# The scan of a state-space layer inside a fused Perceiver kernel: the skip term as a diagonal matrix product, and an output projection in plain float32

## The chip, the cores and the metric

The kernel runs on one core of one Trainium2 chip. The metric is the device time of one execution in microseconds (us). The core has a matrix engine (TensorE, PE in the profile; its weight loads are a row of their own, PEld), a vector engine (VectorE, DVE), a scalar engine (ScalarE, ACT), GpSimd (POOL), and a queue, SyncE (SP), from which this kernel issues all its transfers. Each engine executes its own list of instructions strictly in order and waits on semaphores that the other engines raise. On-chip memory is SBUF; TensorE writes into PSUM.

## The reference, cut to what matters

The input x has 8 sequences of 64 rows of 512 numbers. Six residual blocks follow one another: cross attention over a context of 1601 rows with projections, a mamba block, a ternary linear layer, a second cross attention without weights, a causal self attention, and a gated ternary feed-forward layer. The change touches the mamba block alone:

```
proj = h @ W_in.T ;  x, gate = proj[..., :1024], proj[..., 1024:]
x    = silu(conv4(x))                      # "u" in the kernel
ts, Bm, Cm = rms of the parts of x @ W_x.T
dt   = softplus(ts @ W_dt.T + b_dt) ;  A = -exp(A_log)
for t:  state = state * exp(dt_t * A) + (dt_t * x_t) * B_t ;  y_t = sum_n state * C_t
y    = y + x * D
y    = y * silu(gate)
out  = y @ W_out.T                          # 1024 -> 512
```

The state has 16 components for each of 1024 channels. D is one number for each channel.

## The kernel before, in words

The first cross attention (lines 256 to 604) is by far the largest part and fills the first 2350 us or so. Two sequences make a pair, 128 rows. When a pair has its first cross attention, `chain` (line 782) does the other five blocks for it, as a generator. `run` (line 1312) spreads the chains of the first three pairs over the time of the first cross attention. The chain of the last pair (the "tail", `tail=True`) starts when no cross attention is left, and runs beside what is left of the third pair's chain. So from about 2367 us on there are two chains, that of the third pair and that of the last pair, and the order of their instructions on each engine is set by the framework's list scheduler when the program is built, not by hand.

In the tail all tiles lie in one pool, by tags with a fixed number of buffers: `s4` has 11 (tiles of 4 KB for each partition), `w2` has 12 (2 KB), `w2_r`, which the third pair uses, 8. A tile takes a free buffer of its tag when it is created and gives it back after its last use; a transfer into a tile therefore waits on SP for whoever used the buffer before. Everything behind it on SP waits too.

Mamba in the tail (`mamba`, line 810): channels lie on partitions, in eight chunks c of 128. A chunk's `u[:, c]` is 128 x 128 (channel x 2 sequences of 64 steps). `u` and `dt` and the gate `z` (all chunks of silu(gate), lines 862 to 866) are tiles of tag `s4`, held until the end of the block. Then for each chunk and each group of four state components (`CS = 4`, line 944 to 967):

- ACT makes four exponentials into one of two PSUM buffers `da` (L950),
- POOL (DVE in the first chunk) makes dt * u * B for four components at once, 128 x 512 (L956), into half of a tile `h8` of tag `s4`,
- DVE runs the recurrence (L959), and DVE, or POOL in the second group, multiplies with C (L960),
- PE adds the four components into the PSUM tile `yp[c % 2]` by products with the identity matrix (L962).

`finish(c)` (line 937) then closes a chunk: DVE makes u * D + y (L940), POOL multiplies with the gate (L941), and `mamba_out` (line 989) multiplies with W_out. That product is done in "halves": a float32 number is split into a rounded part and a remainder, both of type fp32r. ACT rounds (L105), DVE subtracts (L106), and `mm3` (line 763) loads the 512-KB pair of halves of W_out from a scratch array `d_wout` into an `s4` tile (L771) and makes three products, high x high (L777), low x high (L778), high x low (L780). They accumulate over the chunks in `wps`. At the end DVE adds the residual (L987).

`mm32` (line 757) is the other way of multiplying that the tail has: it loads a plain float32 matrix into a `w2` tile (L760) and makes one float32 product (L761). The tail's self attention uses it. The names in the profile leave out buffer numbers, so tag `s4` is `s`, the tag `a2` is `a`, and all PSUM tiles of this pool are `acc`.

The third pair's second cross attention runs beside the scan. Its last step, `values` (lines 1077 to 1120), multiplies the weights with the 1601 rows of the context, in 13 tiles; tiles come by six transfers of two (L1099) and a last one of 65 rows (L1101), and the products are L1104. ACT and DVE then close it (L1112, L1113, L1118, L1119). The last pair's second cross attention loads its context tiles into `s4` buffers (L1044).

Of the kernel before, what the change touches and what calls it, by code (L numbers as in the profile page):

```python
# [10 lines left out]
AF = mybir.ActivationFunctionType  # L11
ALU = mybir.AluOpType
# [4 lines left out]
P = 128  # L17
# [12 lines left out]
NCH = 8  # L30
NST = 16
# [47 lines left out]
class Kernel:  # L79
# [730 lines left out]
    def mamba(self, gi, x, xo):  # L810
        nc, i = self.nc, self.i
        tail = self.tail
        lt = self.lnT(x, P, hl=False, tg="a2")
        u = self.sb(self.tv if tail else "lu", [P, NCH, 2, T])
        gs = 2 if tail else 4

        def proj(m):
            w = self.sb(self.tw, [P, NC, P])
            nc.sync.dma_start(out=w, in_=i["W_inT"][m])
            ps = self.acc()  # L820
            for k in range(NC):
                nc.tensor.matmul(ps[:, :P], lhsT=w[:, k, :], rhs=lt(k, 0), start=k == 0, stop=k == NC - 1)  # L822
            return ps[:, :P].rearrange("p (b t) -> p b t", t=T)

        def gate(c, z):
            nc.scalar.copy(z[:, c % 4], proj(NCH + c))
            if c % gs == gs - 1:
                self.silu(z[:, c % 4 - gs + 1 : c % 4 + 1], self.sb("a2", [P, gs, 2, T]), self.sb("a2", [P, gs, 2, T]))

        for c in range(NCH):  # L830
# [4 lines left out]
            uc = u[:, c]  # L835
# [26 lines left out]
        if tail:  # L862
            z = self.sb(self.tv, [P, NCH, 2, T])
# [24 lines left out]
        def bcast(sh):  # L888
            bc = self.sb("bc", [P, 2, HS, 2, T])
            for a in range(2):  # L890
                r = a * NST + sh * HS
                nc.sync.dma_start(
                    out=bc[:, a].rearrange("p s b t -> p (s b t)"),
                    in_=self.bc_s[gi][r : r + HS].rearrange("r t -> (r t)")[None, :].to_broadcast([P, HS * P]),
                )
            return bc

        def scan(c, sh, bc):
            da = self.sb(self.td, [P, HS, 2, T])
            for s in range(HS):  # L900
                k = sh * HS + s
                nc.scalar.activation(da[:, s], dt[:, c], AF.Exp, scale=self.A[:, c, k : k + 1])
            nc.gpsimd.memset(da[:, :, :, 0:1], 0.0)
            du = dus[:, c]
            if sh == 0:
                nc.gpsimd.tensor_tensor(du, dt[:, c], u[:, c], ALU.mult)
            h = self.sb(self.ts, [P, HS, 2, T])
            nc.gpsimd.tensor_tensor(h, bc[:, 0], du[:, None].to_broadcast([P, HS, 2, T]), ALU.mult)

            yield SCAN_COST  # L910
            hf, df = h.rearrange("p s b t -> p (s b t)"), da.rearrange("p s b t -> p (s b t)")
            nc.vector.tensor_tensor_scan(hf, df, hf, 0.0, ALU.mult, ALU.add)
            yield SCAN_COST
            nc.gpsimd.tensor_tensor(h, h, bc[:, 1], ALU.mult)
            yield SCAN_COST
            y = da[:, 0]
            nc.vector.tensor_reduce(y.rearrange("p b t -> p (b t)"), h.rearrange("p s b t -> p (b t) s"), AX.X, ALU.add)
            if sh == 0:
                nc.vector.scalar_tensor_tensor(u[:, c], u[:, c], self.Dp[:, c : c + 1], y, ALU.mult, ALU.add)
            else:  # L920
                nc.gpsimd.tensor_tensor(u[:, c], u[:, c], y, ALU.add)
            yield SCAN_COST

        wps = None
        if tail:


            CS = 4
            bcs = [bcast(sh) for sh in range(nh)]
            das = [self.acc().rearrange("p (s b t) -> p s b t", s=CS, b=2) for _ in range(2)]  # L930
            for da in das:
                nc.scalar.activation(da[:, :, :, 0:1], self.ident[:, : 2 * CS].rearrange("p (s b o) -> p s b o", s=CS, o=1), AF.Copy, scale=0.0)
            hp = self.acc()
            yp = [self.acc() for _ in range(2)]
            wps = self.acc()

            def finish(c):
                uc = u[:, c]
                y = yp[c % 2][:, :P].rearrange("p (b t) -> p b t", t=T)
                nc.vector.scalar_tensor_tensor(uc, uc, self.Dp[:, c : c + 1], y, ALU.mult, ALU.add)  # L940
                nc.gpsimd.tensor_tensor(uc, uc, z[:, c], ALU.mult)  # L941
                self.mamba_out(c, uc, wps)

            for c in range(NCH):
                du = self.sb("du", [P, 2, T])
                nc.gpsimd.tensor_tensor(du, dt[:, c], u[:, c], ALU.mult)
                for k0 in range(0, NST, CS):
                    da = das[k0 // CS % 2]
                    for s in range(CS):
                        nc.scalar.activation(da[:, s, :, 1:], dt[:, c, :, 1:], AF.Exp, scale=self.A[:, c, k0 + s : k0 + s + 1])  # L950
                    bc, o = bcs[k0 // HS], k0 % HS
                    if o == 0:
                        h8 = self.sb(self.ts, [P, HS, 2, T])
                    h = h8[:, o : o + CS]
                    hf = h.rearrange("p s b t -> p (s b t)")
                    (nc.vector if c < HV else nc.gpsimd).tensor_tensor(h, bc[:, 0, o : o + CS], du[:, None].to_broadcast([P, CS, 2, T]), ALU.mult)  # L956

                    eng, hs = (nc.gpsimd, hf) if k0 == CS else (nc.vector, hp)
                    nc.vector.tensor_tensor_scan(hs, da.rearrange("p s b t -> p (s b t)"), hf, 0.0, ALU.mult, ALU.add)  # L959
                    eng.tensor_tensor(hf, hs, bc[:, 1, o : o + CS].rearrange("p s b t -> p (s b t)"), ALU.mult)  # L960
                    for s in range(CS):
                        nc.tensor.matmul(  # L962
                            yp[c % 2][:, :P], lhsT=self.ident, rhs=h[:, s].rearrange("p b t -> p (b t)"), start=k0 + s == 0, stop=k0 + s == NST - 1
                        )
                    if c and k0 == CS:
                        finish(c - 1)
                    yield 15 / 4
            finish(NCH - 1)
        else:
            for sh in range(nh):  # L970
                bc = bcast(sh)
                for c in range(NCH):
                    yield from scan(c, sh, bc)

            wps = self.acc()
            for c in range(NCH):
                if c % 4 == 0:
                    z = self.sb("a2", [P, 4, 2, T])
                gate(c, z)
                yield 0.8  # L980
                if c % 4 == 3:
                    uc = u[:, c - 3 : c + 1]
                    nc.vector.tensor_tensor(uc, uc, z, ALU.mult)
                    for k in range(c - 3, c + 1):
                        self.mamba_out(k, u[:, k], wps)
                        yield 1
# [531 lines left out]
```

## Time and profile before

| what | value |
|---|---|
| runs | 2663.71, 2667.18 (median), 2670.01 us |
| profiled execution | 2656.56 us, of which the span from first to last instruction is 2654.8 us |
| mean granted TensorE clock | 0.984 of full speed |
| busy over the span: PE, DVE, ACT, POOL | 95%, 63%, 51%, 49% |
| the chains' stretch with no first cross attention | 2367 us to the end |
| the last pair's scan | 2419 to 2502 us |
| last pair's L987 (mamba's end) | 2507.33 us |
| last instructions | L1306 of the third pair, after 2651.03 us |

Each row of a view gives a line of the kernel, the engine and the operation. In a timeline the first two numbers are the start in microseconds and the duration of the group; "x8" is the number of instructions in the group, and in brackets stands how long the engine was idle before and who ended that. A float32 product is two records of PE. The view by source line gives, after the count, the shortest, median and longest duration in nanoseconds, then the first and last start in microseconds. The stretch view gives busy microseconds for each engine, the granted clock, the share in which the 16 DMA engines were busy, and GB/s.

### The profile page before, as it was taken

To read this page: it belongs to the slowest core of one execution; us is meant where nothing else is said; L and a number is where in the kernel's file an instruction comes from. 1 tells how busy PE (TensorE), PEld (TensorE's weight loads), DVE (VectorE), ACT (ScalarE), POOL (GpSimd) and SP (SyncE) were. 2 spreads that over 40 slices of the span, in tenths; PEclk is the share of its full clock that TensorE was granted. 3 is DMA by queue.
4 is the path that set the end of the run, shared out by engine and by line. 5 is a ranking of instruction groups with operands and counts; after the bars stand their busy time and mean duration, and the time that the engine had idled before them with its cause. 6 is when DMAs were issued, how large, how long until landed. Compare 5 with 4: busy or idle time off the path is not lost. (4 is left out here: it accounts for less than half of the span.)

```text
span 2654.8 us, 43902 instructions
## 1 busy us (share of the span) xinstructions
PE 2513.8 (95%) x16192; PEld 2241.6 (84%) x16192; DVE 1671.4 (63%) x2747; ACT 1366.8 (51%) x3205; POOL 1291.8 (49%) x1305
## 2 busy tenths in 40 slices
PE   7999999999999999999999989999999999876888
PEld 6999899989989999987989888997898988864545
DVE  4545457665687766544567777554557687668755
ACT  4555554444556555544455555544456555445534
POOL 2445563463378655421356667632138467605420
PEclk9999999999999999999999999999999999987899
DMA  9799776675213244765425533654533543367676
GB/s 300 231 311 301 249 262 202 209 240 168 78 50 108 83 130 138 221 196 152 151 61 163 172 114 97 235 166 146 166 121 107 159 152 122 122 216 240 201 253 227
DMA packets 307672, 466.08 MB, mean 176 GB/s; under 512 B 91129, under 2 KB 187385, under 8 KB 302977
## 3 DMA queue, kind: packets, MB, share of 16 engines
q1 hardware_dynamic: 307456, 463.28, 54.2%
q8 instruction: 127, 2.08, 0.3%
q14 instruction: 89, 0.72, 0.1%
HBM read 389.66 MB, written 73.53 MB: 174 GB/s over the span
## 5 line engine op out<-in xcount | busy, mean ns | idle before, releaser
L367 PE MATMUL k_ps<-cxb,wk 128*128 128x384 f32 x2304 | 463.2, 343 | 28.3 <-ACT cxb L105 10.3
L338 PE MATMUL v_ps<-wv,cxb 128*128 128x256 f32 x3456 | 463.9, 282 | 1.3 <-DVE kt L109 1.2
L338 PEld LDWEIGHTS v_ps<-wv,cxb 128*128 128x128 f32 x3456 | 436.6, 189 | 16.7 <-issue 9.1
L367 PEld LDWEIGHTS k_ps<-cxb,wk 128*128 128x128 f32 x2304 | 399.2, 190 | 48.1 <-ACT cxb L105 10.7
L389 PE MATMUL s_ps<-q,kt 128*128 128x256 f32 (+1 forms) x2496 | 410.9, 298 | 9.6 <-DVE mx L396 4.2
L472 PE MATMUL o_ps<-S,v 128*128 128x256 f32 (+1 forms) x1664 | 409.9, 379 | 0.7 <-ACT v L341 0.4
L389 PEld LDWEIGHTS s_ps<-q,kt 128*128 128x128 f32 (+1 forms) x2496 | 338.9, 185 | 31.2 <-DVE mx L396 5.2
L460 POOL TENSOR_TENSOR ss<-ss,S 128x512 f32<-128x512 f32 x254 | 351.4, 1383 | 13.9 <-ACT S L431 0.9
L392 ACT COPY S<-s_ps 128x512 f32<-128x512 f32 (+1 forms) x448 | 241.8, 553 | 219.7 <-PE s_ps L389 216.2
L396 DVE TENSOR_TENSOR mx<-s_ps,mx 128x512 f32<-128x512 f32 x256 | 175.1, 684 | 285.0 <-ACT S L392 284.3
L472 PEld LDWEIGHTS o_ps<-S,v 128*128 128x128 f32 (+1 forms) x1664 | 298.7, 189 | 34.1 <-issue 1.4
L433 POOL TENSOR_TENSOR ss<-S,S 128x512 f32<-128x512 f32 x64 | 83.7, 1308 | 424.7 <-ACT S L431 377.0
L430 DVE TENSOR_TENSOR S<-S,m_ps 128x512 f32<-128x512 f32 (+1 forms) x448 | 257.8, 640 | 19.6 <-PE m_ps L416 19.4
L431 ACT ACTIVATE S<-S 128x512 f32<-128x512 f32 (+1 forms) x448 | 247.0, 600 | 44.3 <-DVE S L430 44.1
L108 ACT ACTIVATE kt<-k_ps,c_bk 128x384 fp32r<-128x384 f32 (+1 forms) x256 | 151.8, 593 | 211.9 <-PE k_ps L367 211.3
L109 DVE SCALAR_TENSOR_TENSOR kt<-k_ps,c_bk,kt 128x384 fp32r<-128x384 f32 (+1 forms) x256 | 160.7, 628 | 132.3 <-ACT kt L108 131.7
L341 ACT COPY v<-v_ps 128x256 f32<-128x256 f32 (+1 forms) x416 | 151.7, 368 | 162.2 <-PE v_ps L338 157.9
L338 PE MATMUL v_ps<-wv,cxt 128*128 128x256 f32 (+1 forms) x1536 | 208.6, 285 | 3.4 <-DVE kt L109 2.5
L338 PEld LDWEIGHTS v_ps<-wv,cxt 128*128 128x128 f32 (+1 forms) x1536 | 194.2, 177 | 12.9 <-DVE kt L109 3.8
L65 DVE TENSOR_TENSOR_SCAN a<-a,a 128x512 f32<-128x512 f32 x96 | 153.8, 1603 | 66.2 <-POOL a L65 66.0
L367 PE MATMUL k_ps<-cxt,wk 128*128 128x450 f32 x768 | 177.6, 374 | 0.3 <-ACT v L341 0.3
L65 ACT ACTIVATE a<-lv,c_A_log 128x128 f32<-128x128 f32 x384 | 123.2, 393 | 101.6 <-DVE a L65 100.8
(382 smaller groups left out, 3969.9 us busy)
## 6 DMA issues: line engine op xcount, KB each, us to landing
wo<-d_wo SPq DMA_DIRECT2D x127, 512.0 KB, 5.5
wk<-d_wk SPq DMA_DIRECT2D x63, 512.0 KB, 3.8
wv<-d_wv SPq DMA_DIRECT2D x31, 1024.0 KB, 5.8
cst<-in_ctxT_dram SPq DMA_DIRECT2D x96, 192.0 KB, 2.9
d_q<-q_t SPq DMA_DIRECT2D x32, 512.0 KB, 5.1
q<-d_q SPq DMA_DIRECT2D x64, 256.0 KB, 2.8
d_wo<-wo SPq DMA_DIRECT2D x32, 512.0 KB, 5.0
w<-d_wat SPq DMA_DIRECT2D x64, 256.0 KB, 3.3
```

Of the source, the lines that this page charges most:

```text
L65: return lambda *a, **k: self.tc.keep_in_program_order(f(*a, **k))
L108: nc.scalar.activation(hi, src, AF.Identity, bias=bias)
L109: eng.scalar_tensor_tensor(lo, src, bias, hi.bitcast(FP), ALU.add, ALU.subtract)
L338: nc.tensor.matmul(ps[:r], lhsT=cx[:, a, c, o : o + r], rhs=w[:, m, c, :], start=k == 0, stop=k == 11)
L367: nc.tensor.matmul(ps[:, :wd], lhsT=w[:, a, c, :], rhs=cx[:, m, c, :], start=k == 0, stop=k == 11)
L389: nc.tensor.matmul(sp[:r, gi, :], lhsT=kt[:, a, o : o + r], rhs=q[:, m, :], start=k == 0, stop=k == 2)
L392: nc.scalar.copy(s[:r, :n], sp[:r, :n])
L396: nc.vector.tensor_tensor(mx, sp, S[0] if len(S) == 1 else mx, ALU.max)
L430: nc.vector.tensor_tensor(sv, sv, ps[:r, 1:2].to_broadcast([r, w, 256]), ALU.add)
L431: nc.scalar.activation(sv, sv, AF.Exp, scale=ISC)
L460: nc.gpsimd.tensor_tensor(ss, ss, S[n], ALU.add)
L472: nc.tensor.matmul(ps[:, 0], lhsT=self.v[(b, j, t)][:r, hc : hc + P], rhs=S[t // 2][:r, t % 2], start=t == 0, stop=t == NT - 1)
```

## The change

Three things change, all in the last pair's mamba alone. First, eight diagonal matrices are made at the start of the block, chunk by chunk, by ACT from the identity and D, in a tile `dg` of tag `s4` (eight instructions of 128 x 128). Second, D u is added by PE: before a chunk's first group of states, a float32 product of the diagonal matrix with `u[:, c]` opens the sum in `yp`, and the sixteen products with the identity follow. `finish` no longer adds u * D on DVE and no longer multiplies on POOL; one DVE instruction multiplies y, read from PSUM, with the gate. Third, W_out is multiplied by `mm32`: no rounding on ACT, no subtraction on DVE, one float32 product in place of three fp32r products, and a 256-KB transfer into a `w2` tile in place of 512 KB into an `s4` tile. The first three pairs are computed as before.

```diff
@@ mamba
         gs = 2 if tail else 4
+        if tail:
+            dg = self.sb(self.tv, [P, NCH, P])
+            for c in range(NCH):
+                nc.scalar.activation(dg[:, c], self.ident, AF.Copy, scale=self.Dp[:, c : c + 1])
@@ finish
                 y = yp[c % 2][:, :P].rearrange("p (b t) -> p b t", t=T)
-                nc.vector.scalar_tensor_tensor(uc, uc, self.Dp[:, c : c + 1], y, ALU.mult, ALU.add)
-                nc.gpsimd.tensor_tensor(uc, uc, z[:, c], ALU.mult)
-                self.mamba_out(c, uc, wps)
+                nc.vector.tensor_tensor(uc, y, z[:, c], ALU.mult)
+                self.mm32(wps, uc.rearrange("p b t -> p (b t)"), i["W_outT"][c], c == 0, c == NCH - 1)
@@ the loop over groups of states
                     bc, o = bcs[k0 // HS], k0 % HS
+                    if k0 == 0:
+                        nc.tensor.matmul(yp[c % 2][:, :P], lhsT=dg[:, c], rhs=u[:, c].rearrange("p b t -> p (b t)"), start=True, stop=False)
@@
-                            yp[c % 2][:, :P], lhsT=self.ident, rhs=h[:, s].rearrange("p b t -> p (b t)"), start=k0 + s == 0, stop=k0 + s == NST - 1
+                            yp[c % 2][:, :P], lhsT=self.ident, rhs=h[:, s].rearrange("p b t -> p (b t)"), start=False, stop=k0 + s == NST - 1
```

## The prediction, made before the changed kernel ran

> **What bounds the kernel now.** I read the stretches first, to see which engine is full where the change acts.
>
> ```profile
> core 0: us, PE busy (x) PEld busy (x) DVE busy (x) ACT busy (x) POOL busy (x), PEclk, DMA share, GB/s
> 2425.00:2497.00 72.00, 60.73 (x375) 42.56 (x376) 68.37 (x100) 51.02 (x155) 51.83 (x53) 0.90 0.48 155
> 2497.00:2510.00 13.00, 8.21 (x41) 4.85 (x40) 7.32 (x15) 3.20 (x10) 3.33 (x5) 0.81 1.09 326
> ```
>
> In the scan DVE is busy 68.4 of 72 us (95%), PE 84%, ACT 71%, POOL 72%, the DMA engines 48%. In its last 13 us no engine is full, and the DMA engines are. So the scan is paced by DVE, and its end by something else. What that is, the chain of waits from 2485 to 2526 us says (start, length, what):
>
> ```profile
> 2494.58 1.03 PE acc L1104 x4
> 2495.61 0.02 issue
> 2495.63 7.73 DMA b_r<-in_ctxN_dram
> 2503.36 0.04 issue
> 2503.41 1.09 PE acc L1104 x2
> 2504.49 0.02 issue
> 2504.52 0.58 ACT b L1112
> 2505.10 0.21 ACT a L105
> 2505.31 0.04 issue
> 2505.35 0.80 PE acc L777
> ...
> 2506.87 0.44 PE acc L780
> 2507.31 0.02 issue
> 2507.33 0.69 DVE xr L987
> ...
> 2515.80 4.12 DMA w_r<-d_wat
> 2519.92 0.02 issue
> 2519.94 5.80 DMA w_r<-d_wat
> ```
>
> The third pair's last context tile (L1101) lands at 2503.36, one us after the last state sum (L962) ended at 2502.29. PE takes L1104 before the last W_out products, and ACT takes L1112 before the last rounding L105, so both chains wait for that tile. Later two loads of d_wat hold PE before the last pair's second cross attention, whose L1047 starts at 2526.93. Rows for the prices, from the views by source line:
>
> ```profile
> L106 DVE TENSOR_TENSOR a<-s,a x8: 273/292/1179, 2445.8 to 2505.7; 128x128 fp32r<-128x128 f32 x8
> L940 DVE SCALAR_TENSOR_TENSOR s<-s,c_Dp,acc x8: 314/322/349, 2438.7 to 2502.3; 128x128 f32<-128x128 f32 x8
> L836 ACT ACTIVATE s<-xpad,c_conv_b,c_conv_w x8: 481/494/495, 2375.7 to 2384.1; 128x128 f32<-128x128 f32 x8
> ```
>
> **The change part by part**, with the order that the two programs' instructions have on each engine.
>
> *Diagonal matrices.* Eight ACT instructions, 128 x 128, SBUF to SBUF with a scale per partition. No such row exists. Below: four casts of the same size take 0.90 us together (L65, 2359.13), so 8 x 0.225 = 1.8 us. Above: L836, with scale and bias, is 0.49 alone, 3.9 us. Four exponentials of 126 columns with a scale per partition (L950) take 1.57 us in a row, 0.39 each: I take 3.1 us. They stand on ACT ahead of the block's first L118, and wait for the third pair's last W_out product, since the pool's memory is free only then; SP's first weight load waits for the same and starts at 2367.42. So they end at 2369.2, 2370.5 or 2371.3, and L118 (2369.51) comes 0, 1.0 or 1.8 us later; behind it wait the layer norm, its transposes and all projections. What hides that: u is complete at 2391.12 (L748), but its last product L850 stands on PE behind L1047, which waits for a context tile until 2391.24 and ends at 2392.3. So up to 1.1 us costs nothing. On SP one 256-KB load of d_wat now stands before that tile's transfer (issued 2385.29, 5.91 us to landing, DMA share 1.06): 0.25 MB at 375 GB/s is 0.7 us. These overlap; I take **+0.7** (0 to +1.8).
>
> *The scan.* DVE loses eight L106; six lie before the last exponentials (2497.8): 0.28 + 1.18 + 0.87 + 0.42 + 0.29 + 0.29 = 3.3 us. The new product reads PSUM and SBUF as L960 does, 0.69 us for 512 columns; L940 of the same 128 columns is 0.32, and I leave the product there. A gain of 0.2 more from one operand fewer is possible. Bounds: 6 x 0.28 = 1.7 us if the long ones were long only because POOL was in the way and the next instruction inherits that, 3.9 us with all eight. I take **-3.4**.
>
> The Trainium skill's page "SBUF — State Buffer", section "Who interferes with whom", says that a DVE instruction with two SBUF inputs and a GpSimd one that reads SBUF exclude each other, and one with a PSUM input does not. L106 (two SBUF inputs: 273 to 1179 ns) against L940 (one in PSUM: 314 to 349 ns) agrees. By the rule the whole 3.3 goes; by the short row alone it would be 1.7.
>
> ACT loses 8 x 0.28, POOL 8 x 0.45 us; neither paces. PE changes three fp32r products of 512 columns (0.23 apart: 2.1) for one float32 product: eight records of L761 take 3.44 us, two make a product, 0.86. The diagonal is a 128-column float32 product, 0.23 (L822: eight records, four products, in 0.98). Per chunk 0.86 + 0.23 - 0.69 = +0.4, in all +3.2 us, hidden by PE's 72.0 - 60.7 = 11.3 us of idle time; without that cover +3.2. W_out's 2 MB instead of 4 come early, in `w2` buffers, so `h8` has seven buffers to itself where it shared eight with W_out; POOL's wait of 3.7 us for L780 (L956, 2447.43) goes. SP's attnT loads (eight) and d_ffn (four), which came before 2412, move behind W_out's, into the scan and its end.
>
> *The end of the scan.* Let E be the end of the last exponentials, 2497.76 before. L1101 now stands on SP behind a load that takes `dt`'s buffer and so waits for E, then an attnT and one more load: issue at about E + 1.1, where it was E - 2.1. Context loads from 2478 to 2508 land after 3.6 us in the median case, this one took 7.73: E + 4.7 to E + 8.8, before E + 5.6. The other b_r loads have 4.9: I take E + 6.0, **+0.4** (-0.9 to +3.2). From its landing to L987 it was 3.97 us. Now L1104 1.09, then the last W_out product, which has its operands: 0.86 at full clock, 1.72 at half, and some 0.15 until DVE starts: 2.1 to 3.0. PE was at half clock there (L777, L778 of 0.80, 0.72 against 0.40). I take **-1.1** (-1.9 to -1.0).
>
> *Behind it.* The last pair's ffn products (eight) now stand before the third pair's d_wat products, and of those only the 12 with loads made early and two groups more (four loads) stand before L1047, where seven loads had to land. Four loads' landing is at 2519.9 in the chain, the seventh 2525.7. But the d_wat loads are issued about 2 us later (behind ffn and four attnT loads), and ffn's result must go through another layer norm (L794 at 2519.33 to L736 at 2523.56 before). So L1047 comes 0 to 3.6 us earlier beyond what it inherits; I take **-2.0**. The end comes after a stretch bound by PE and loads; I let the sum through.
>
> Sum: 0.7 - 3.4 + 0.4 - 1.1 - 2.0 = **-5.4 us** against the profiled execution, 2656.56 to 2651.2. The median of the runs lies 10.6 us above that execution; the same step gives 2667.18 - 5.4 = **2661.8 us**. Within 0.2% (5.3 us) a measurement of this kernel can hardly tell a change from none, its three runs being 6.3 us apart.
>
> **Rivals.**
>
> A, the forecast: most terms come out. Its own range, with the ends of the terms that go together, is -10 (0 - 3.9 - 1.9 - 0.9 - 3.6) to -3, 2657 to 2664.
>
> B, the context tile holds the end and nothing is gained behind it. For it: the chain runs through that tile and not through DVE, and the third pair, which depends on it, ends the run. Against: the tile's place on SP follows E, which comes earlier. Price: 0.7 - 3.4 + 3.2 - 1.0 = -0.5, 2666.7 us.
>
> C, slower: the loads moved from before the scan become the bound at its end. Between E and the first d_wat load seven attnT loads (1.75 MB) are issued, before none. At 326 GB/s they take 5.4 us of DMA time, before loads that the third pair waits for, and L1101 lands at its late end. Price: 0.7 - 3.4 + 3.2 - 1.0 + 5.4 = +4.9; with PE's +3.2 no longer covered by waits, +8.1: about +6.5, 2673.7 us. It decides if the DMA engines have no gap from E to the d_wat loads. For it: their share of 1.09. Against: in the DMA view of 2508 to 2530 (40 slices of 0.55 us) they stood still for six slices, 3.3 us, just before those loads:
>
> ```profile
> GB/s 339 356 298 304 343 237 56 11 0 0 0 0 0 0 134 358 350 242 253 305 276 291 302 317 387 380 376 387 406 406 413 402 376 384 402 376 399 376 395 306
> ```
>
> **How the numbers follow.** A 0.60, B 0.16, C 0.24. A centres on the limit of 0.2% and its longer arm is the gain, since each stretch that ends sooner also keeps PE's clock up: 0.50 of it faster, 0.10 within. B is nearly all within (0.11), 0.02 faster, 0.03 slower. C is slower 0.23, within 0.01. Faster 0.52, same 0.22, slower 0.26. The range goes from below A (2654) to C (2674).
>
> **What would show it.** Right: DVE's busy time in the scan down by 3 us with no new idle time; the scan's E to L987 not longer than 9.6 us; L1047 of the last pair before 2523. Wrong at once: L1104's last tile landing later than E + 7; POOL or DVE waiting for PE at L761 in the scan; a L118 later than 2371 with u late for L850; or d_wat loads landing after 2526.

## The result: slower by 0.3%, and the profile after

Twenty runs of each kernel, taken beside each other, gave medians of 2661.46 us before and 2669.57 us after; the ratio is 1.0032, with a 95% interval of 1.0021 to 1.0043. The forecast was 5.4 us faster; measured are 8.1 us slower. The profiled execution took 2667.86 us (span 2665.2), 11.3 us more than that of before. Lines of the changed kernel carry other numbers: those from 816 to 939 of before stand 4 further down, those from 943 to 951 3 further, those from 952 on 5 further (L959 is L964, L1047 is L1052, L1104 is L1109, L1253 is L1258).

The stretches of the changed kernel, over the same times as in the prediction (us, busy us of each engine with its instructions, granted clock, DMA share, GB/s):

```profile
core 0: us, PE busy (x) PEld busy (x) DVE busy (x) ACT busy (x) POOL busy (x), PEclk, DMA share, GB/s
2425.00:2497.00 72.00, 57.70 (x357) 41.58 (x358) 66.10 (x93) 50.29 (x148) 49.88 (x47) 0.85 0.40 124
2497.00:2510.00 13.00, 11.62 (x61) 6.52 (x59) 4.48 (x7) 1.54 (x5) 1.27 (x1) 1.00 1.09 336
```

DVE lost 2.3 us of work, as intended, and PE lost 3.0 us in the scan and gained 3.4 behind it: in the last 13 us it is busy for 11.6, where it was for 8.2. The chain of waits of the changed kernel over the same end (start, length, what):

```profile
2484.34 0.70 DVE s L965
2485.04 0.14 issue
2485.18 2.05 PE acc L967 x8
2487.22 1.15 PE acc L1091 x9
2488.38 4.02 PE acc L1109 x12
2492.40 5.55 PE acc L967 x48
2497.95 1.00 PE acc L1109 x2
2498.95 1.05 PE acc L761 x2
2500.01 0.22 PE acc L956 x2
2500.23 0.89 PE acc L967 x8
2501.12 1.02 PE acc L1109 x3
2502.14 0.02 issue
2502.16 6.82 DMA b_r<-in_ctxN_dram
2508.97 0.14 issue
2509.11 1.06 PE acc L1109 x2
...
2523.76 6.29 DMA w_r<-d_wat
```

Before, the chain lay mostly on DVE and ACT until 2486.8, then on PE until the context tile was issued at 2495.63 (those lines stand below, with the scan), and on the tile through the end. Now PE carries it from 2485 to 2502, and the tile comes later: it is issued 3.2 us after the last exponentials (these end at 2498.93), when PE's products L1109 give back its buffer, and lands 10 us after them. The rows by source line that answer to L940 and L106 (shortest, median, longest in ns, first and last start), and the new one of the diagonal matrices:

```profile
L944 DVE TENSOR_TENSOR s<-acc,s x8: 265/279/292, 2440.2 to 2506.8; 128x128 f32<-128x128 f32 x8
```
```profile
L819 ACT ACTIVATE s<-ident,c_Dp x8: 385/386/401, 2366.7 to 2368.8; 128x128 f32<-128x128 f32 x8
```

One execution is not the kernel. I divided the tail of each profiled execution at the starts of seven instructions: the first and the last scan step (L959), the mamba's end (L987), the last pair's first transposes for its second cross attention (L1086), the first product of its self attention (L761), the end of its self attention (its L1253, the second one), and the last L1306. Zero is the first instruction of the last pair's mamba on POOL (L833), which waits for the third pair's last W_out product. The table, worked out from those starts, also holds the experiments; "e8" is the kernel before, profiled again. The third pair's self attention ends with the first L1253; its distance from L1086 is the last column.

```
                                  scan  scan  mamba's                 2nd                     L1086 to
                                 first  last   end    L1086   L761   L1253   end    total   3rd L1253
before                           55.2   75.7    9.0   31.5    32.7   42.1   37.4   283.6     45.2
e8 before again                  58.7   75.9    8.8   33.3    32.7   43.5   38.1   291.0     45.2
e4 reorder only                  57.1   75.3    9.4   32.1    32.7   42.5   37.3   286.3     45.2
the change                       57.6   74.9   12.1   30.1    36.9   45.4   37.7   294.7     51.7
e9 the change, 1 copy            58.9   76.4   12.2   28.0    37.2   50.3   39.3   302.3     60.7
e10 the change, 2 copies         59.6   75.1   13.4   30.2    32.5   41.7   50.5   303.1     45.1
e5 the change, 2 copies in tiles 62.3   76.4    8.2   30.9    32.9   42.5   38.7   291.9     45.4
e1 W_out only                    57.7   76.1    6.7   29.2    36.9   49.7   38.2   294.6     61.2
e12 W_out only, 2 copies         55.6   76.2    8.2   29.6    32.4   41.4   49.9   293.3     45.0
e2 diagonal only                 59.3   78.2    6.0   31.1    37.9   43.7   38.6   294.9     52.5
e3 change, W_out in s4           57.7   75.7    7.1   29.7    37.6   44.3   38.9   291.0     52.6
e11 change, W_out in s4, 2 copies 59.2  75.1    8.5   32.3    32.9   42.7   37.5   288.2     45.4
e6 the same, copies in tiles     63.8   81.6    9.6   29.6    32.7   42.8   38.2   298.4     45.2
e7 before, third pair delayed    57.0   75.2    8.6   28.2    37.8   49.9   37.4   294.1     62.2
```

Two things stand out. The execution that the prediction was made from was a short one: the same program gave 291.0 another time, and most of the difference lies in the steps that wait for loads. So a row of this table is one execution, and only differences beyond that spread count. And the columns behind L1086 take few values: 32.4 to 32.9 or 36.9 to 37.9, 41.4 to 45.4 or 49.7 to 50.3, 37 to 39 or 50.

### The profile page after: what moved, and what is told of

Its sections match the earlier page's. It is cut to its first block, busy times and chain, and to the rows that moved or that the text cites. A ratio compares the mean times of both kernels' runs of the same rounds, so it can differ in the third digit from the quotient of the medians.

```text
span 2665.2 us, 43905 instructions
## 1 busy us (share of the span) xinstructions
PE 2524.2 (95%) x16200; PEld 2251.0 (84%) x16200; DVE 1666.7 (63%) x2739; ACT 1370.1 (51%) x3205; POOL 1289.5 (48%) x1297
## 4 chain that ended last, share of the span: by engine, by line
PE 68%; DVE 10%; DMA 8%; POOL 7%; ACT 4%; issue 3%; SPq 0%; POOLq 0%; DVEq 0%; ACTq 0%
PE k_ps L367 16%; PE v_ps L338 16%; PE o_ps L472 9%; PE s_ps L389 8%; DVE a L65 3%; POOL a L65 3%; PE acc L278 3%; PE w_ps L522 2%; PE acc L826 2%; PE acc L1109 2%; PE acc L777 2%; POOL ss L460 2%; PE acc L1052 1%; PE acc L778 1%; DVE b L65 1%
## 5 line engine op out<-in xcount | busy, mean ns | idle before, releaser
L367 PEld LDWEIGHTS k_ps<-cxb,wk 128*128 128x128 f32 x2304 | 403.1, 192 | 46.3 <-ACT cxb L105 10.4
```

The lines of the kernel that those rows point to most:

```text
L367: nc.tensor.matmul(ps[:, :wd], lhsT=w[:, a, c, :], rhs=cx[:, m, c, :], start=k == 0, stop=k == 11)
```

## The experiments

Four theories. P: the float32 product makes PE the bound at the scan's end. S: the loss begins with the diagonal matrices at the block's start and goes through. L: the loads that W_out's early loads displace. O: the order that the scheduler finds. In what follows ffn is the ternary linear layer behind the mamba, the K products are the first ones of the third pair's self attention (they read the d_wat loads), the attnT products belong to the last pair's self attention, and d_gu holds matrices of the gated feed-forward layer.

**One part alone.** e1 takes W_out alone (in `finish` of before, `self.mamba_out(c, uc, wps)` becomes the line with `self.mm32`); e2 the rest alone:

```diff
                 nc.vector.tensor_tensor(uc, y, z[:, c], ALU.mult)
-                self.mm32(wps, uc.rearrange("p b t -> p (b t)"), i["W_outT"][c], c == 0, c == NCH - 1)
+                self.mamba_out(c, uc, wps)
```

> Only W_out as one plain float32 product per chunk; D u and the gate as before. Theory P (the float32 product makes TensorE the bound at the scan's end, and the third pair's last context tile is loaded late because of it): most of the loss, +4 to +7 us against before (ratio 1.0015 to 1.0026), TensorE over 85% busy from 2495 to 2508, the last context tile issued over 3 us after the last exponentials. Theory S (the loss begins with the diagonal matrices at the block's start and goes through): -3 to +1 us. Theory L (the displaced loads): +5 to +8 us, since W_out's loads stand early here too.

> Only D u by the diagonal product and the gate on VectorE; W_out in halves as before. P: 0 to +3 us (TensorE has +0.23 us a chunk, no more). S: +5 to +8 us, the scan starting 1.7 us late as in the changed kernel. L: 0 to +2 us, since W_out's loads are the old ones.

e1: 1.0031 (1.0018 to 1.0043), +8.2 us. e2: 1.0038 (1.0023 to 1.0052), +9.9 us. Each half costs what both cost together, so neither P, S nor L holds as a price of one part. e1's 8.2 us lie just above P's range and L's, and PE is 88% busy from 2495 to 2508, as P said. But the place is another: its last context tile is issued 5.8 us before the last exponentials end (2499.41 and 2505.24), its mamba ends 2 us sooner after the scan than before's and its L1086 comes at 169.8 us, among the earliest; all of its loss, and more, lies behind.

**Loads and order.** e3 is the change with W_out's tiles from `s4` (`mm32` gets the tag as an argument); e4 is the kernel before with another yield.

```diff
-                self.mm32(wps, ..., c == NCH - 1)
+                self.mm32(wps, ..., c == NCH - 1, "s4")
```
```diff
-                    yield 15 / 4
+                    yield 17 / 4
```

> The whole change, but W_out's 256-KB loads go into the s4 tiles, as the 512-KB ones did, so that the attnT and ffn loads keep their early places. L: the loss is gone (-2 to +2 us). P: the loss stays (+6 to +9 us). S: the loss stays, and the scan starts 1.0 to 1.8 us late.

> The kernel before, computing the same with the same instructions, with another weight in the interleaving of the scan (yield 17/4 for 15/4), which changes only the order. P, S and L: within 1.5 us of before. Theory O (the order that the scheduler happens to find is worth several us by itself): 3 us or more in either direction.

e3: 1.0017 (1.0005 to 1.0030), +4.2 us: about half of the loss remains, which none of the theories had. Its mamba ends about 1.7 us or more sooner after the scan than before's (7.1 against 8.8 to 9.4), so the long step at the scan's end that the change has isn't there in this version with the same products. e4: 1.0003 (0.9989 to 1.0017). O as I put it, that any other order costs microseconds, isn't seen here; but this version's order on DVE behind the mamba, and on SP throughout, is that of before.

That led to theory O2: the loss arises behind the mamba, from the order there. In the changed kernel and in e1, e2 and e3 the scheduler takes the last pair's ffn before the third pair's K products, in before and e4 behind them. On PE, after the eight transposes L730:

```
before, e4:            L777 L778 L780 (third pair, K) x4, then L777 L778 (last pair, ffn) x4
the change, e1 to e3:  L777 L778 (last pair, ffn) x4, then L777 L778 L780 (third pair, K) x4
```

**Forcing the order.** e5 and e6 put two copies of the W_out sum on the path, so that the mamba ends later and the K products come first; e7 does the reverse to the kernel before.

```diff
+        if tail:
+            for eng in (...)[:2]:
+                w = self.sb("b2", [P, D])
+                (nc.scalar.copy if eng[0] == "s" else nc.gpsimd.tensor_copy)(w, wps)
+                wps = w
         nc.vector.tensor_tensor(xo, wps, x, ALU.add)
```
```diff
+            if bs[0] == 4 and k == 1:
+                for _ in range(1):
+                    tc = self.sb("b2", [T, D])
+                    nc.scalar.copy(tc, ta)
+                    ta = tc
             if q0 == 0:
```

> The whole change, with two needless copies of the last pair's W_out sum (one on ScalarE, one on GpSimd, some 1.6 us together) ahead of the residual, which make the mamba end later and so let the scheduler put the third pair's K products before the last pair's ffn products again, as in the kernel before. Theory O2 (the loss arises behind the mamba, from the order ffn first): although work is added on the path, faster than the whole change: +1 to +4 us against before (ratio 1.0004 to 1.0015), the last pair's first attnT products (line 761) at full clock. Theory P (the loss arises in the scan, from TensorE): +9 to +11 us, later by the copies.

> The kernel with W_out's loads in s4 tiles, with the same two copies. O2: -2 to +2 us against before (3 to 5 us less than without the copies). P: +5 to +7 us.

> The kernel before, nothing of the change in it, with one needless copy (64 x 512 on ScalarE, 0.6 us) at the end of the third pair's second cross attention, which makes the scheduler choose the order ffn first. O2: slower by 4 to 8 us, as the changed kernels are. P: within 1 us of before (0.6 for the copy).

> The kernel before once more, to see how far the places of its steps move from one profiled execution to the next. All theories: the tail, from the third pair's last W_out product to the last line 1306, within 1 us of 283.6 if its profile was typical; some 286 if that profile was a short one.

e7: 1.0026 (1.0015 to 1.0037), +7.3 us. Up to the mamba's end its orders on PE, DVE and SP are those of before, to the instruction, but for the third pair's closing L1119, which changes places with L987 on DVE; one copy of 0.6 us and the order behind it cost nearly what the whole change costs. In the table it gains up to L1086 (28.2 against 31.5 to 33.3) and loses 5 and 7 us after. e5: 1.0005 (0.9991 to 1.0020), +2.5 us, as O2 said. The whole change with work added is faster than without. With each set against the runs of before beside it, the difference is 5.6 us by the medians and 0.27% (7 us) by the ratios, whose intervals just don't overlap. e6: 1.0038 (1.0021 to 1.0055), +9.8 us, against O2 and above P's range too. The table shows why: behind L1086 it has before's values (32.7, 42.8, 38.2), but its scan takes 81.6 us and starts late. Two more `b2` tiles had changed the orders long before the mamba's end; this holds for e5 too. e8 gave 291.0, beyond both values that were expected: one program's steps spread more than I had allowed.

**The same without another tile.** In e9 to e12 the copies go from the sum onto itself, so that every order up to the mamba's end stays as it was without them (but for L1119, and L141 in e12, which DVE takes ahead of L987 in e10 to e12).

```diff
+        if tail:
+            for _ in range(2):
+                nc.scalar.copy(wps, wps)
         nc.vector.tensor_tensor(xo, wps, x, ALU.add)
```

> The whole change with one needless copy on ScalarE (the W_out sum onto itself, 128 x 512 in PSUM, 0.6 us) ahead of the residual; all engines' orders are those of the changed kernel up to there, and behind it the last pair's ffn still stands first, in the variant that the experiment with W_out alone and the one with the third pair delayed had. Theory O2 (the order behind the mamba): as slow as the change or slower, +8 to +13 us against before. Theory P (the loss arises in the scan): +8 to +9.

> As the last, with two such copies (1.2 us): again all orders are the changed kernel's up to the mamba's end, but behind it the third pair's K products stand first, as in the kernel before. O2: faster than the change and than the version with one copy, +1 to +4 us against before; from the last pair's first cross-attention transposes to its first attnT products (lines 1086 to 761) about 32.8 us instead of 37. P: +9 to +10.

> W_out's loads in s4 tiles, with two copies; VectorE's order behind the mamba is the kernel before's to the last instruction. O2: -2 to +2 us against before (without the copies it was +4.5). P: +5 to +6.

> W_out alone as a float32 product (D u and gate as before), with two copies, K products first. O2: -3 to +2 us against before (without the copies it was +8). P: +9.

e9: 1.0046 (1.0029 to 1.0062), +12.2 us, as O2 said. e11: 1.0000 (0.9986 to 1.0013), by the medians 4 us better than e3 with 1.2 us of copies more (the two intervals still overlap); it is the one whose order on DVE behind the mamba is before's to the last instruction. e10: 1.0054 (1.0034 to 1.0075), +13.3 us, and e12: 1.0045 (1.0029 to 1.0061), +9.3 us, are both against O2. e12's number is P's, but its mamba ends no later after the scan than before's (8.2 us, with the copies). In both the K products come first and the two steps behind L1086 are as short as before's (74 us together against 75 to 76). But then the last step takes 50 us. The two pairs end far apart; here the last two L1306 of before, and those of e10 (where the line is 1314):

```profile
2648.11 0.75 DVE L1306 SCALAR_TENSOR_TENSOR xr<-acc,s_oct,xr 128x512 f32<-128x512 f32 x1 [1.01 <-PE acc L778]
2651.03 0.75 DVE L1306 SCALAR_TENSOR_TENSOR xr<-acc,s_oct,xr 128x512 f32<-128x512 f32 x1 [1.52 <-PE acc L778]
```
```profile
2669.07 0.75 DVE L1314 SCALAR_TENSOR_TENSOR xr<-acc,s_oct,xr 128x512 f32<-128x512 f32 x1 [5.17 <-PE acc L778]
2679.49 0.75 DVE L1314 SCALAR_TENSOR_TENSOR xr<-acc,s_oct,xr 128x512 f32<-128x512 f32 x1 [2.59 <-PE acc L778]
```

2.9 us apart in the one, 10.4 in the other: the last feed-forward steps of the two pairs stand in another order, and the third pair ends far behind. So O2 was too narrow, and is mended: it isn't the place of the K products alone but the whole order behind the mamba. This mended form was made after e10 and e12; no run was forecast with it. But the traces bear it out. From the first d_wat load behind the mamba on, SP issues its transfers in just four orders, and PE's order goes with them (the same to the instruction within a row, but for the third):

```
order behind the mamba                                       L1086 to the end
before's: before, e8, e4, e5, e6, e11                        112.2 to 114.2
ffn first: the change, e2, e3                                120.0 to 120.8
ffn first, d_gu loads in another order: e1, e7, e9           124.8 to 126.8
K products first, another order at the end: e10, e12         123.7 to 124.7
```

Each row mixes versions with and without parts of the change, and none of the later rows comes near the first. So what comes behind L1086 goes with the order and not with the arithmetic. Since the orders of SP and of the engines change together, which of them costs how much isn't shown.

What isn't settled either: an early mamba's end together with before's order, without the copies that brought it about, was not had; from e11 less its 1.2 us it would be within 0.1% of before, too little to be told apart. Nothing here beats the kernel before.

## Why the prediction was wrong, by its own steps

The step that decided is the last one, "I let the sum through": by the profiles 7.0 us of the loss arise there, behind L1086. Two more failed ahead of it: "the scan is paced by DVE", which promised 3.4 us, and the landing of the context tile, put at 6.0 us after the last exponentials and measured at 10.0.

**The diagonal matrices (+0.7, bounds 0 to +1.8).** The price of one was right: 0.386 us against 0.39. But eight in a row took 2.45 us, not 3.1, and L118 came only 0.23 us later in every version that has them (2.28 against 2.05 after zero). What they cost together with the load ahead of the context tile is the first column: 57.6 to 59.6 in the six versions with them (without e5 and e6, whose order there is another), mean 58.7; 55.2 to 58.7 in the six without, mean 56.9. So about +1.9, at the upper bound, though with 3.4 us between two executions of one program that size is not certain. My cover, the context tile, itself landed later, and PE had gone to half clock while it waited (the products take 1.97 us instead of 1.08): the eight L1047 of before and after, from PE's timeline (in brackets the idle time before):

```profile
2391.24 1.08 PE L1047 MATMUL acc<-b,b 128*64 128x256 f32 x8 [0.68 <-DMA b<-in_ctxT_dram]
```
```profile
2392.08 1.97 PE L1052 MATMUL acc<-b,b 128*64 128x256 f32 x8 [1.91 <-DMA b<-in_ctxT_dram]
```

**The scan (-3.4).** DVE's work went down as forecast, from 71.9 to 69.0 us between the first and last scan step, and L944 took 0.28 us, below my 0.32. The time did not: 75.2 to 75.9 us without the change, 74.9 to 76.4 with it. The step that failed is "the scan is paced by DVE", and with it that the scan gains what DVE loses. It was read from DVE's busy share, 95%. The chain of waits before, of which the prediction shows only the end, leaves DVE some 13 us before the context tile is issued, for ACT's exponentials of the third pair's softmax and then for PE:

```profile
2481.27 1.23 DVE acc L959
2482.50 0.01 DVE s1m L1067
2482.51 0.02 issue
2482.54 0.37 ACT acc L950
2482.91 2.15 ACT b L1070 x6
...
2488.30 2.73 PE acc L1104 x12
```

What DVE waited for in the scan, by the view of waits (us in total, times, longest), before and then after:

```profile
DVE acc L959 <- ACT acc L950: 1.8, 3, 0.7
DVE a L106 <- ACT a L105: 0.8, 1, 0.8
```
```profile
DVE acc L964 <- ACT acc L953: 3.0, 3, 1.7
DVE s1s L1077 <- ACT s1x L1075: 0.9, 1, 0.9
DVE s L964 <- ACT acc L953: 0.7, 1, 0.7
```

It now waits 3.7 us for exponentials, and in all it is idle for 5.9 us between the first and last scan step, where it was for 3.8. The longest such wait, with what stood ahead on ACT, from the two engines' timelines of the changed kernel:

```profile
2487.88 0.37 ACT L1093 COPY b<-acc 128x256 f32<-128x256 f32 x1 [1.07 <-PE acc L1091]
2488.15 0.38 ACT L953 ACTIVATE acc<-s,c_A_log 128x126 f32<-128x126 f32 x1
```
```profile
2489.86 1.23 DVE L964 TENSOR_TENSOR_SCAN acc<-acc,s 128x512 f32<-128x512 f32 x1 [1.74 <-ACT acc L953]
```

ACT's copy of the third pair's transposes waits for PE, the exponentials stand behind it, and DVE behind them. PE was late in part because it ran at half clock, after little work (eight L967 take 2.05 us at 2485.18 and 1.06 at 2475.78), in part because it had itself waited for ACT (1.44 us, L1075) and DVE (0.59 us):

```profile
2476.00:2480.00 4.00, 2.37 (x22) 1.92 (x20) 4.00 (x7) 2.59 (x7) 4.00 (x4) 1.00 0.71 187
2480.00:2484.00 4.00, 2.24 (x5) 1.07 (x6) 3.92 (x9) 3.51 (x11) 4.00 (x5) 0.59 0.52 178
2484.00:2488.00 4.00, 3.41 (x20) 3.03 (x21) 2.40 (x5) 2.90 (x11) 2.18 (x2) 0.50 0.07 28
```

A W_out product (L761) had kept PE waiting 1.87 us, until 2480.31, for the gate's product on DVE. In the second row the clock falls to half with PE busy 2.2 of 4 us. The Trainium skill's page "TensorE: Matmul & The Clock Gate", section "What's actually happening", puts the fall to half clock after an idle window of about 3.4 us; the longest idle time of PE in these rows is 1.87 us, so the measurement goes further than the page.

**PE's +3.2, hidden by 11.3 us of idle time.** This cover failed in the whole change: the idle time that was left lay early, the work came late, and from the last scan step to L987 PE was busy for 10.5 of 12.1 us, where it had been for 7.0 of 9.0. That is +2.9 us (12.0 in the mean of the change, e9 and e10 less their copies, against 9.1 in that of before, e8 and e4) where the steps at the scan's end together were forecast at -0.7. With the same products and W_out's tiles in `s4` (e3, e11) the step is some 1.8 us shorter than before, so it isn't the arithmetic but the order of instructions and loads. In the terms of the sum, the tile was to land at E + 6.0 (4.7 to 8.8) and landed at E + 10.0: its issue was to follow E by 1.1 us, with SP's order alone in view, and followed it by 3.2, since the tile's buffer came free only with PE's L1109. From its landing to L987 it took 2.4 us, as forecast (2.1 to 3.0). Of the loads that were to move into the scan, five attnT loads were issued there (2441 to 2482); the four d_ffn loads came ahead of it, at 2406 to 2410. In PE's price three fp32r products count 0.69 us, as the sum has it; the 2.1 beside them enters no sum.

**Behind it (-2.0).** At L1047, for which it was forecast, little of it came: L1047 starts 19.1 us after L987 in the change, 19.6 to 19.8 in before, e8 and e4, so -0.5. Only four d_wat loads had to land, as I had it, but the first was issued 11.0 us after L987 and not 7.6, 3.4 us later where I had counted 2, and the fourth landed 18.6 us after L987 (2530.05), when before the seventh had landed after 18.4. Up to L1086 the gain is of the forecast size: the change, e9 and e10 take 28.0 to 30.2 us from L987 where before, e8 and e4 take 31.5 to 33.3. Whether the ffn products ahead of the K products do it isn't shown: e7 has nothing of the change but that order and takes 28.2, but e10 and e12, with the K products first, take 30.2 and 29.6. That the size up to L1086 fits is luck, then.

**"I let the sum through."** This is the step that decided. I saw that ffn moves ahead of the third pair's K products and counted it as a gain for the last pair, without asking what the third pair, which ends the run beside it, then waits for. Its self attention ends 51.7 us after L1086 instead of 45.2. Part of it is again PE's clock. The last pair's transposes and first attnT products in before, then in the change:

```profile
2569.54 0.66 PE L730 MATMUL acc<-ident,b 128*128 128x128 f32 x4 [0.38 <-DVE b L144]
2571.04 0.66 PE L1217 MATMUL acc<-ident,b 128*128 128x128 f32 x4 [0.84 <-POOL b L1209]
2571.53 3.60 PE L761 MATMUL acc<-w,b 128*128 128x512 f32 x8
```
```profile
2575.96 0.85 PE L730 MATMUL acc<-ident,b 128*128 128x128 f32 x4 [2.50 <-DVE b L144]
2577.53 1.11 PE L1222 MATMUL acc<-ident,b 128*128 128x128 f32 x4 [0.72 <-POOL b L1214]
2578.44 5.93 PE L761 MATMUL acc<-w,b 128*128 128x512 f32 x8
```

PE has nothing left to do while DVE works through the layer norm between the third pair's softmax steps, and then runs eight products in 5.93 us instead of 3.60. That is 2.3 of the 6.5 us; the others had come up before these products start (36.9 us after L1086, not 32.7), and what makes them isn't followed further here. The third pair's last products stand behind them, and the d_gu loads behind those. Against the mean of before, e8 and e4, the change's own row gives +0.6 to the first scan step, -0.7 in the scan, +3.1 at its end, -2.2 to L1086 and +7.0 from there (120.0 against 113.0): +7.7, beside the 8.1 us between the medians. Nine tenths of it lie behind L1086. The rest, +0.7 over four steps, is less than one program's spread; the 7.0 are not, since before's order gives 112.2 to 114.2 in six profiles.

**The rivals.** B's mechanism was real (the context tile held the scan's end, 10 us behind the last exponentials where I had allowed 8.8), and two of my signs for "wrong at once" came: that tile later than E + 7, d_wat loads landing at 2530 instead of 2526 or sooner. C had the right sign and a time near the measured one, but the wrong cause. The DMA engines did stand still before the d_wat loads; over 2495 to 2525 in 40 slices of 0.75 us, in the change:

```profile
GB/s 358 311 335 382 374 369 345 350 345 330 329 342 347 339 310 232 274 350 336 359 352 345 165 94 277 393 306 14 0 0 0 0 0 22 197 249 309 339 314 194
```

Six slices, 4.5 us, are nearly empty, so those loads weren't bound by bandwidth. And e1, with W_out's early loads, and e2, without them, lose alike. So C's nearness in time is luck.

## What to carry to other kernels

Where a scheduler orders the instructions, a change in one block can also turn the order of what follows it, and that may be worth more than the change: here 7 to 14 us behind L1086, and in e7 for no more than one copy of 0.6 us. So compare the order behind the edit too, ask of each swap which chain ends the run, and test it by a needless copy onto itself at the block's end, which here left nearly all orders ahead of it alone. And an engine that is busy for 95% of a loop isn't its only limit if the engines that feed it wait for each other: in the change 2.9 us less work on DVE came with 2.2 us more waiting.

## What I had not expected of the hardware

The granted clock fell to half without a long pause of PE: around 2480.7 in the change, where PE had some 1.5 us of work in the 3.4 us before and no pause longer than 1.9 us, and again around 2576.3, with some 0.9 us of work and a pause of 2.5 us. And one program's steps that wait for loads differ by up to 3.4 us from one execution to the next (55.2 and 58.7 to the first scan step), while those bound by the engines agree within 0.3 us (75.7 and 75.9 in the scan, 32.7 and 32.7 behind L1086).
